# A spectral convolution and a cosine-like convolution on NHWC images: layer 1 with fixed homes for its blocks, an engine order tied to the step, and image statistics in thirds

## The chip, the cores and the metric

The kernel runs on one core of one Trainium2 chip. The metric is device time in microseconds (us), from one launch of the whole kernel. A core has five engines that run side by side, each through its own queue of instructions in a fixed order: TensorE (PE, with its weight loads shown apart as PEld), VectorE (DVE), ScalarE (ACT), GpSimd (POOL), and SyncE (SP), which here only issues DMAs. Engines wait for one another through semaphores. Data comes from DRAM into SBUF by DMA; PE writes its results to PSUM.

## The reference, cut to what matters

The input x has the shape (4, 512, 512, 16), float32. Two layers are added to it, each on a group-normalised input (8 groups of 2 channels, mean and variance over the whole image).

```python
# layer 0: a rational filter applied by a 1024 x 1024 FFT
x = x + _L0_conv_ref(_gn(x), L0_conv_h0, L0_conv_numerators, L0_conv_denumerator)
# layer 1: a 3 x 3 convolution, normalised like a cosine, through arccos
x = x + _L1_conv_ref(_gn(x), L1_conv_kernel, L1_conv_bias, L1_conv_radius)
...
    input_norm = sqrt(conv(x * x, ones) + EPS)        # 3 x 3 x C sum of squares
    kernel_norm = sqrt(sum(kernel * kernel) + EPS)
    y = conv(x, kernel / kernel_norm) / input_norm    # 'SAME'
    y = 1.0 - arccos(y) * (2.0 / pi)
    y = y * (tanh(kernel_norm / radius) * tanh(input_norm / radius))
    return y + bias
```

Only the end of layer 0 and layer 1 matter here.

## The kernel before, in words

The phases follow one another: filter, forward transform, the mixing of channels in the frequency domain, and `last_phase`, which holds the inverse transform along w, the statistics of layer 1, and layer 1 itself.

**The inverse transform.** 16 tiles of 16 rows each (256 row steps). A row step does eight matmuls into two PSUM tiles (lines 1163 and 1166), a copy on ACT (1169), two additions on POOL (1171 and 1172), three instructions on DVE (1173, 1176, 1177), and a DMA to DRAM. PSUM tiles have three buffers.

**The image statistics, `prepare`.** A generator that other loops advance by one stage at a time. It goes over the 64 places of 128 x 128 pixels (16 for each image), loads x (`p_x`, 1 MB) and layer 0's result (`p_y0` and `p_y1`, 0.5 MB each, eight channels in each) one place ahead, adds them on POOL (line 1098), takes one `bn_stats` for each channel on DVE (line 1094), and stores the sum (`t_d`). A place takes three calls: the add of channels 0 to 7; the add of channels 8 to 15 with the statistics of 0 to 7; the statistics of 8 to 15 with the store. After an image's 16 places come 16 aggregates and a chain of small operations through two matmuls, which leave the scale and shift `vec` of the image, in three more calls. The inverse transform calls it once every two row steps in its last seven tiles, so 56 times; 204 calls are needed in all.

**Layer 1.** An image is cut into groups of 32 columns (`xt`, 512 x 32 x 16), 16 for each image, 64 in all. A group has four blocks of 8 columns by 16 channels, with h in the free dimension (`block`: four transposes on PE, then Identity with scale and shift on ACT into `xn`, and Square into `x2`), and four units of 128 rows (`conv`: twelve matmuls over the group's four blocks and one for the columns of the neighbouring groups; each float32 matmul makes two records in the trace). There are 256 blocks and 256 units. A block has 512 elements and a zero on each side, which are the image's upper and lower border.

A step u of the loop works on many stages at once; what it issues, with line numbers, in the order of the code:

- `squares(u+13)`: four small matmuls of `x2` (1237) into one PSUM tile with a single buffer, and a copy to `sums` on DVE (1241), with copies on POOL of a group's outer column into its neighbour's (1243, 1246);
- every fourth step `norms`: three matmuls (1258 to 1260), the root and, every eighth step, tanh on ACT (1265, 1267; each change between tanh and the root loads a function table), a reciprocal on DVE (1269);
- `block(u+14)`: transposes (1211), the memset of the two border elements on POOL (1217), Identity (1219), Square (1221);
- every fourth step `border`: two copies on POOL (1287), four transposes (1290), two memsets on POOL, three instructions on DVE (1299);
- `conv(u+3)` (1307, 1315);
- `signed(u)` on POOL (1353) and `finish(u-1)`, the last addition on POOL (1367) with the output's DMA;
- `root(u+1)` (Abs, Relu, Sqrt; 1331 to 1333), `gate(u+1)` on POOL (1348), `factors(u+1)` (three squares and Sign; 1341 and 1343);
- `chain(u)`: five dependent instructions on DVE (1359 three times, 1360, 1362); the last one frees the unit's PSUM tile, of which there are four;
- `cosine(u+2)` on DVE (1325);
- every fourth step `over_w` on POOL (1250, 1251); then one call of `prepare`, if u is not negative.

The loop runs from u = -14 (`lead` is 14) to 256.

**What sets the order.** The framework records all instructions and then schedules them: each engine's queue is filled by a list scheduler that takes, among what it holds to be ready by its own estimate of time, what stands first in the program. So an instruction can be moved ahead of others that stand before it in the code. `InOrder` (line 213) is a helper that the kernel already uses in its filter phase: inside its `with` block, each instruction of the engines that it was given gets an edge from the one before it on the same engine, without a semaphore, so that the scheduler keeps the order of the code there. In layer 1 nothing is tied before the change. A tile from a pool is given to a buffer when one is free; the next tile in the same buffer waits for the last reader of the former.

```python
np_ = ctx.enter_context(tc.tile_pool(name="l_xn", bufs=16))
...
xn = np_.tile([P, N + 2], F32, name="xn")
nc.gpsimd.memset(xn[:, 0 : N + 2 : N + 1], 0.0)
vec = vecs[order[q // 64]]
nc.scalar.activation(xn[:, 1 : N + 1], pt, AF.Identity, scale=vec[:, 0:1], bias=vec[:, 1:2])
```

Of the kernel before, what the change touches and what calls it, by code (L numbers as in the profile page):

```python
# [40 lines left out]
F32 = mybir.dt.float32  # L41
# [5 lines left out]
P = 128  # L47
N = 512
# [160 lines left out]
def bc(ap, axis, shape):  # L209
    return ap.unsqueeze(axis).to_broadcast(shape)  # L210
# [758 lines left out]
def last_phase(tc, cst, x, y_d, yw_d, t_d, kern, bias, radius, out):  # L969
    nc = tc.nc  # L970
    with ExitStack() as ctx:
# [94 lines left out]
        def prepare():  # L1066


            places = [(b, w, h) for b in order for w in range(4) for h in range(4)]

            def load(b, w, h):
                t = pp.tile([P, P, C], F32, name="p_x")
                nc.sync.dma_start(out=t, in_=x[b, h * P : (h + 1) * P, w * P : (w + 1) * P, :])
                ys = []
                for jh in range(2):
                    y = pp.tile([P, C // 2, P], F32, name=f"p_y{jh}")
                    nc.sync.dma_start(
                        out=y, in_=yw_d[b][jh * C // 2 : (jh + 1) * C // 2, h * P : (h + 1) * P,
                                           w * P : (w + 1) * P].rearrange("j h w -> h j w"),
                    )  # L1080
                    ys.append(y)
                return t, ys

            ahead = load(*places[0])
            for at, (b, w, h) in enumerate(places):
                t, ys = ahead
                if w == 0 and h == 0:
                    stats = sm.tile([P, C, 16, 6], F32, name="l_stats")
                if at + 1 < len(places):
                    ahead = load(*places[at + 1])  # L1090

                def half(jh):
                    for j in range(8 * jh, 8 * jh + 8):
                        nc.vector.bn_stats(stats[:, j, 4 * w + h, :], t[:, :, j])

                def add(jh):
                    part = t[:, :, 8 * jh : 8 * jh + 8]
                    nc.gpsimd.tensor_add(part, part, ys[jh].rearrange("p j w -> p w j"))

                add(0)  # L1100
                yield
                add(1)
                half(0)
                yield
                half(1)
                nc.sync.dma_start(out=t_d[b][w][h * P : (h + 1) * P], in_=t)
                yield
                if w < 3 or h < 3:
                    continue

                mc = sm.tile([P, C, 2], F32, name="l_mc")
                for j in range(C):
                    nc.vector.bn_aggr(mc[:, j, :], stats[:, j].rearrange("p n s -> p (n s)"))
                nc.vector.tensor_sub(mc[:, :, 0], mc[:, :, 0], bias_b)
                pair = mc.rearrange("p (g k) s -> p g k s", k=2)
                mv = joined(nc, sm, pair[:, :, 0, :], pair[:, :, 1, :])
                mu = sm.tile([P, 8], F32, name="gn_mu")
                nc.vector.tensor_copy(mu, mv[:, :, 0])
                yield
                pm = ps_s.tile([P, 8], F32, name="gn_ps", tag="gn_ps")  # L1120
                nc.tensor.matmul(pm, mean_m, mu, start=True, stop=True)
                mean = sm.tile([P, 8], F32, name="gn_mean")
# [12 lines left out]
                nc.vector.scalar_tensor_tensor(both[:, 1], mean, -1.0, both[:, 0], ALU.mult, ALU.mult)  # L1135

                vec = sm.tile([P, 2], F32, name="l_vec", bufs=B)
                nc.vector.tensor_mul(both, both, bc(group, 1, [P, 2, 8]))
                nc.vector.reduce_sum(vec, both, axis=AX.X)
                nc.vector.scalar_tensor_tensor(vec[:, 1:2], vec[:, 0:1], bias_n, vec[:, 1:2],  # L1140
                                               ALU.mult, ALU.add)
                vecs[b] = vec
                yield
# [3 lines left out]
        with inner:  # L1147
            for n in range(16):
                b2, half, s8 = n // 8, n // 4 % 2, n % 4
# [33 lines left out]
                        next(beside, None)  # L1183

        xp = ctx.enter_context(tc.tile_pool(name="l_x", bufs=8))
        np_ = ctx.enter_context(tc.tile_pool(name="l_xn", bufs=16))
        ew = ctx.enter_context(tc.tile_pool(name="l_ew", bufs=2))
        ps_t = ctx.enter_context(tc.tile_pool(name="l_pst", bufs=2, space=PSUM))
        ps_c = ctx.enter_context(tc.tile_pool(name="l_psc", bufs=4, space=PSUM))
# [3 lines left out]

        n_groups = 16 * B
        n_units = 4 * n_groups
        borders, xt, xns, x2s, sums, pcs, rins, ths, st = ({} for _ in range(9))
        sh = [P, 32, C]

# [8 lines left out]
        def block(q):  # L1207

            pt = ps_t.tile([P, N], F32, name="pt")
            for h in range(4):  # L1210
                nc.tensor.transpose(
                    pt[:, h * P : (h + 1) * P],
                    xt[q // 4][:, h, q % 4 * 8 : q % 4 * 8 + 8, :].rearrange("p w c -> p (w c)"),
                    ident,
                )
            xn = np_.tile([P, N + 2], F32, name="xn")
            nc.gpsimd.memset(xn[:, 0 : N + 2 : N + 1], 0.0)
            vec = vecs[order[q // 64]]
            nc.scalar.activation(xn[:, 1 : N + 1], pt, AF.Identity, scale=vec[:, 0:1], bias=vec[:, 1:2])
            x2 = ew.tile([P, N], F32, name="x2")  # L1220
            nc.scalar.activation(x2, xn[:, 1 : N + 1], AF.Square)
            xns[q], x2s[q] = xn, x2
# [9 lines left out]
        def squares(q):  # L1232

            g, k = q // 4, q % 4
            p2 = ps_s.tile([P, 4, 8], F32, name="p2", tag="gn_ps")
            for h in range(4):
                nc.tensor.matmul(p2[:, h], x2s[q][:, h * P : (h + 1) * P], cols, start=True, stop=True)
            del x2s[q]
            if g not in sums:
                edges(g)  # L1240
            nc.vector.tensor_copy(sums[g][:, :, 1 + 8 * k : 9 + 8 * k], p2)
            if k == 0 and g % 16 > 0:
                nc.gpsimd.tensor_copy(sums[g - 1][:, :, 33:34], sums[g][:, :, 1:2])
            if k == 3 and g % 16 < 15:
                edges(g + 1)
                nc.gpsimd.tensor_copy(sums[g + 1][:, :, 0:1], sums[g][:, :, 32:33])
# [30 lines left out]
                    hi = 32 if ql == 0 and dh == 0 else min(8 * ql + 9, 32)  # L1277
                    yield 4 * g + ql, dh, lo, hi, lo - (8 * ql - 1)

        def border(g):  # L1280

            t = ew.tile([P, 4, 3, 2, C], F32, name="e_bx")
            for side in range(2):
                at, w = (g + 2 * side - 1, 31 - 31 * side)
                if at // 16 != g // 16 or at < 0:
                    at, w = g, 0
                nc.gpsimd.tensor_copy(t[:, :, :, side], bc(xt[at][:, :, w, :], 2, [P, 4, 3, C]))
            pt = ps_t.tile([P, N], F32, name="pt")
            for h in range(4):
                nc.tensor.transpose(pt[:96, h * P : (h + 1) * P],  # L1290
                                    t[:, h].rearrange("p d s c -> p (d s c)"), ident)
            bx = ew.tile([96, N], F32, name="e_bn")
            nc.gpsimd.memset(bx[0:32, 0:1], 0.0)
            nc.gpsimd.memset(bx[64:96, N - 1 : N], 0.0)
# [28 lines left out]
        def cosine(u):  # L1323
            y = ew.tile(sh, F32, name="e_y", bufs=4)
            nc.vector.tensor_mul(y, pcs[u], bc(rins[u // 4][:, u % 4, :], 2, sh))  # L1325
            st["y", u] = y
# [44 lines left out]
        lead = 14  # L1371

        def step(u):
# [7 lines left out]
                norms(g)  # L1381
            if u + lead < n_units:
                block(u + lead)
            if u % 4 == 2 and 0 <= u + 6 < n_units:
                border((u + 6) // 4)
            if 0 <= u + 3 < n_units:
# [8 lines left out]
                factors(u + 1)  # L1395
            if 0 <= u < n_units:
                chain(u)
            if 0 <= u + 2 < n_units:
                cosine(u + 2)
            g, k = divmod(u + lead - 2 - 4, 4)  # L1400
            if k == 0 and 0 <= g < n_groups:
                over_w(g)
# [6 lines left out]
            next(beside)  # L1409
        for g in range(3):  # L1410
            load(g)
        for u in range(-lead, n_units + 1):
            step(u)


def body(tc, ins, cst, out):
# [47 lines left out]
```

## Time and profile before

| | us |
|---|---|
| median of three runs | 16199.08 (16192.73 to 16224.64) |
| the profiled execution, its own time | 16219.56 |
| its span, first to last instruction | 16217.8 |
| inverse transform without statistics, 13600 to 13800 | 73 row steps |
| inverse transform with statistics, 13800 to 14300 | 148 row steps |
| first block of layer 1 (line 1211) | 14387.8 |
| first instruction of chain(0) (line 1359) | 14436.6 |
| last statistics load issued (line 1073) | 15467.5 |
| end of the span | 16217.8 |

Over the whole span PE is busy 91%, DVE 66%, ACT 55%, POOL 65%, at a mean granted clock of 0.969. Layer 1 is only its last ninth: of 40 slices of 405 us it fills the last four and a half. Times inside the trace are counted from the start of the span. A line of the trace gives its start, its length, the engine, the source line, the operation, the tiles (what is written, an arrow, what is read), the shape and the number of instructions merged into the line. Lengths of neighbouring records overlap by up to 0.1 us, since an engine starts the next instruction before the last one's end is recorded; so the distance between starts tells what an instruction costs. In a list of waits, a line names the engine and line that waited, the one that it waited for, the sum in us, how often, and the longest.

### The profile page before, as it was taken

The page shows a single profiled execution, that of the slowest core. Times are in us where ns is not written, and L with a number is a line of the kernel's source. Part 1 is how long each engine was busy: PE and PEld are TensorE (multiplying, and loading weights), DVE is VectorE, ACT ScalarE, POOL GpSimd, SP SyncE. Part 2 cuts the span into 40 slices and gives each one's busy share as a digit, 9 for nine tenths or more (in the row PEclk, how much of TensorE's full clock was granted, in tenths as well). Part 3 has the DMA queues.
Part 4 walks back from the last instruction along what each step waited for, and adds up shares of the span by engine and source line. Part 5 has one row for each costly group of instructions (what it writes and reads, how often), then busy time and mean ns, then how long its engine had stood idle before and what let it go on. Part 6 is the DMA issues. An engine that isn't in the chain of part 4 may idle for free. (4 is left out here: it accounts for less than half of the span.)

```text
span 16217.8 us, 539020 instructions
## 1 busy us (share of the span) xinstructions
PE 14720.9 (91%) x232588; PEld 10874.5 (67%) x232588; DVE 10679.6 (66%) x21019; ACT 8839.0 (55%) x17007; POOL 10556.5 (65%) x10157
## 2 busy tenths in 40 slices
PE   7999999999988888888888888888888889888898
PEld 5555555554557666667676676677676767777787
DVE  8999999993545555555555555555555555778877
ACT  4666666663345555555555555555555553147788
POOL 7777777772356666666666666666666665667766
PEclk8999999999999999999999999999999999989899
DMA  4888888888878888888888888888888888975521
GB/s 138 239 244 246 244 245 239 244 242 259 251 271 329 326 330 329 330 329 326 329 327 328 330 327 329 326 324 330 329 329 330 328 330 305 326 253 196 197 103 66
DMA packets 2917339, 4542.72 MB, mean 280 GB/s; under 512 B 125730, under 2 KB 2094076, under 8 KB 2805262
## 3 DMA queue, kind: packets, MB, share of 16 engines
q1 hardware_dynamic: 2705758, 3836.11, 68.6%
q0 software_dynamic: 172336, 605.00, 9.4%
q10 hardware_dynamic: 36864, 67.13, 1.2%
q8 instruction: 1830, 29.98, 0.7%
q14 instruction: 551, 4.51, 0.1%
HBM read 3030.45 MB, written 1477.31 MB: 278 GB/s over the span
## 5 line engine op out<-in xcount | busy, mean ns | idle before, releaser
L848 PEld LDWEIGHTS pm<-xe,gh 128*32 128x32 f32 x131328 | 1996.9, 111 | 1437.8 <-issue 1141.2
L848 PE MATMUL pm<-xe,gh 128*32 128x64 f32 x131328 | 2366.9, 222 | 649.6 <-issue 320.2
L832 PE MATMUL pg<-c_dg,g 64*128 64x128 f32 x32832 | 2607.1, 290 | 311.9 <-ACT gh L732 195.8
L877 DVE TENSOR_TENSOR z<-zq,pz 128x256 f32<-128x256 f32 x2052 | 860.0, 419 | 2956.7 <-ACT zq L876 2952.5
L832 PEld LDWEIGHTS pg<-c_dg,g 64*128 64x128 f32 x32832 | 2143.6, 191 | 575.4 <-ACT gh L732 245.2
L732 ACT COPY gh<-pg 128x512 f32<-128x512 f32 x2567 | 1447.8, 585 | 1302.8 <-PE pg L832 1299.9
L462 PE MATMUL pt<-ev_in,c_todd 128*128 128x512 f32 x4096 | 1924.9, 609 | 9.1 <-DMA ev_in<-g_d 9.0
L392 DVE RECIPROCAL dn<-dn 128x256 f32<-128x256 f32 x1024 | 1722.9, 1724 | 17.6
L393 POOL TENSOR_TENSOR sp<-m,dn 128x512 f32<-128x512 f32 x1024 | 1301.4, 1271 | 592.0 <-DVE dn L392 555.2
L812 ACT COPY xe<-xl 64x1024 f32<-64x1024 f32 x513 | 539.0, 1051 | 1868.9 <-POOL xl L803 1868.9
L730 DVE COPY gh<-pg 128x512 f32<-128x512 f32 x1537 | 1055.4, 687 | 661.0 <-PE pg L832 658.4
L869 PE MATMUL pz<-c_ident,yf 128*128 128x128 f32 x8208 | 1378.5, 291 | 18.5 <-issue 11.6
L801 POOL TENSOR_TENSOR xu<-xe,c_late 128x256 f32<-128x256 f32 x2052 | 1374.5, 694 | 21.7 <-DVE xe L730 6.9
L462 PEld LDWEIGHTS pt<-ev_in,c_todd 128*128 128x128 f32 x4096 | 729.1, 190 | 909.9 <-issue 772.9
L421 ACT COPY st<-pg 128x256 f32<-128x256 f32 x2048 | 617.0, 390 | 1300.9 <-PE pg L410 1300.9
L410 PEld LDWEIGHTS pg<-c_dinv,sp 64*128 64x128 f32 x16384 | 1005.5, 196 | 442.1 <-ACT sp L398 232.6
L803 POOL TENSOR_TENSOR xl<-xl,xu 128x1024 f32<-128x1024 f32 x513 | 1209.2, 2357 | 40.2
L1307 PE MATMUL pc<-l_band,xn 128*128 128x160 f32 (+2 forms) x6144 | 1112.8, 341 | 70.7 <-DVE e_o L1362 70.1
L410 PE MATMUL pg<-c_dinv,sp 64*128 64x128 f32 x16384 | 1108.1, 287 | 60.3 <-ACT sp L398 44.6
L885 POOL TENSOR_TENSOR zd<-z 128x512 f32<-128x512 f32 x513 | 654.5, 1276 | 778.8 <-DVE z L877 778.8
L917 POOL DMA_DIRECT2D y_d<-yo x511 | 296.5, 580 | 1275.9 <-ACT yo L732 1250.3
L906 PE MATMUL py<-z,c_ig 128*64 128x256 f32 x6156 | 1120.5, 396 | 6.5 <-issue 2.7
(216 smaller groups left out, 30900.2 us busy)
## 6 DMA issues: line engine op xcount, KB each, us to landing
xe<-xf_d SPq DMA_DIRECT2D x1026, 1536.0 KB
g<-g_d SPq DMA_DIRECT2D x511, 1024.0 KB
g_d<-st SPq DMA_DIRECT2D x256, 1024.0 KB
ev_in<-g_d SPq DMA_DIRECT2D x1024, 256.0 KB
g_d<-ot SPq DMA_DIRECT2D x1024, 256.0 KB
xf_d<-xe POOLq DMA_DIRECT2D x513, 448.0 KB, 8.2
xf_d<-xl POOLq DMA_DIRECT2D x513, 448.0 KB, 6.3
x_d<-xo SPq DMA_DIRECT2D x128, 1024.0 KB
```

The costliest lines, as they stand in the source:

```text
L392: nc.vector.reciprocal(dn, dn)
L393: nc.gpsimd.tensor_mul(w["sp"][:, v], w["m"][:, v], bc(dn, 2, [P, 2, 2, P]))
L410: nc.tensor.matmul(pg[u][:, n, k].rearrange("p a x -> p (a x)"), w["sp"][q, n, k, c, :], dinv[q, 2 * kp + k, c, :], start=(c == 0), stop=( ...
L462: nc.tensor.matmul(pt, todd[:, c, kc, hh * P : hh * P + P], ev[:, kc, c], start=(kc == 0), stop=(kc == 1),)
L732: nc.scalar.copy(dst, src)
L801: nc.gpsimd.tensor_mul(u[:, :, h, c], xe[:, :, h, 1 - c], bc(late[:, 1 + c], 2, [P, F, 2]))
L803: nc.gpsimd.tensor_add(xl.rearrange("p f h c k -> p (f h c k)"), xl.rearrange("p f h c k -> p (f h c k)"), u.rearrange("p f h c k -> p (f ...
L832: nc.tensor.matmul(pg[c][:, j % 4], g[half, j], dg[half], start=True, stop=True)
L848: nc.tensor.matmul(pm[32 * q : 32 * q + 32, g % 8], gh[:, f].rearrange("p c j -> p (c j)"), xe[:, :, f].rearrange("p t h c k -> p t (h c k ...
L869: nc.tensor.transpose(pz[:, t % 4].rearrange("p v q x -> p (v q x)"), y[:, at].rearrange("p g x -> p (g x)"), ident)
L906: nc.tensor.matmul(py[64 * half : 64 * half + 64, odd], ig[:, s0, c2], zs.rearrange("p (t h) j -> p h t j", h=2), start=(c2 == 0), stop=(c ...
L1307: nc.tensor.matmul(pc[:, lo:hi, :].rearrange("p w j -> p (w j)"), xns[q][:, h * P + dh : h * P + dh + P], bands[dh][:, o : o + hi - lo, :] ...
```

## The change

- The 16 homes of normalised blocks become 16 tiles of their own, made once, and their border elements are set to zero once. `block(q)` writes into home q modulo 16. The 256 memsets become 16.
- Every step of layer 1's loop is put into an `InOrder` block for PE, DVE, ACT and POOL. SP is left to the scheduler.
- Three helpers are cut in two, so that a part can stand elsewhere in the step: the POOL copies of `border` become `ends`, one step earlier; the memsets and DVE rows of `border` become `borders_in`, after `chain`; the neighbour copies of `squares` become `across`, after `cosine`.
- A place of the statistics is cut into 6, 5 and 5 channels in place of 8 and 8. The adds of a place are 0 to 5; 6 to 7 and 8 to 10; 11 to 15. The statistics are 0 to 5, 6 to 10 and 11 to 15, each one call after its add; the last third falls into the first call of the next place. The store stays in the third call.

```diff
-                add(0)
+                add(0, 6)
                 yield
-                add(1)
-                half(0)
+                add(6, 8)
+                add(8, 11)
+                sums(0, 6)
                 yield
-                half(1)
+                add(11, 16)
+                sums(6, 11)
                 nc.sync.dma_start(out=t_d[b][w][h * P : (h + 1) * P], in_=t)
                 yield
+                sums(11, 16)
...
-        np_ = ctx.enter_context(tc.tile_pool(name="l_xn", bufs=16))
+        np_ = ctx.enter_context(tc.tile_pool(name="l_xn", bufs=1))
...
+        ring = [np_.tile([P, N + 2], F32, name=f"xn{n}") for n in range(16)]
+        for t in ring:
+            nc.gpsimd.memset(t[:, 0 : N + 2 : N + 1], 0.0)
...
-            xn = np_.tile([P, N + 2], F32, name="xn")
-            nc.gpsimd.memset(xn[:, 0 : N + 2 : N + 1], 0.0)
+            xn = ring[q % 16]
...
+
+        def across(q):
+            g, k = q // 4, q % 4
             if k == 0 and g % 16 > 0:
                 nc.gpsimd.tensor_copy(sums[g - 1][:, :, 33:34], sums[g][:, :, 1:2])
...
+            if u % 4 == 1 and 0 <= u + 7 < n_units:
+                ends((u + 7) // 4)
             if u % 4 == 2 and 0 <= u + 6 < n_units:
                 border((u + 6) // 4)
...
             if 0 <= u < n_units:
                 chain(u)
+            if u % 4 == 2 and 0 <= u + 6 < n_units:
+                borders_in((u + 6) // 4)
             if 0 <= u + 2 < n_units:
                 cosine(u + 2)
+            if 0 <= u + lead - 1 < n_units:
+                across(u + lead - 1)
...
+        tied = InOrder(tc, nc.tensor, nc.vector, nc.scalar, nc.gpsimd)
         for u in range(-lead, n_units + 1):
-            step(u)
+            with tied:
+                step(u)
```

More of the change, by code (lines that the diff above doesn't have):

```diff
@@ L1090, in prepare, with sums, add @@
                     ahead = load(*places[at + 1])
-                def half(jh):
-                    for j in range(8 * jh, 8 * jh + 8):
+                def sums(lo, hi):
+                    for j in range(lo, hi):
                         nc.vector.bn_stats(stats[:, j, 4 * w + h, :], t[:, :, j])
-                def add(jh):
-                    part = t[:, :, 8 * jh : 8 * jh + 8]
-                    nc.gpsimd.tensor_add(part, part, ys[jh].rearrange("p j w -> p w j"))
-                add(0)
+                def add(lo, hi):
+                    jh = lo // 8
+                    part = t[:, :, lo:hi]
+                    nc.gpsimd.tensor_add(part, part, ys[jh][:, lo - 8 * jh : hi - 8 * jh].rearrange("p j w -> p w j"))
+                add(0, 6)
                 yield
-                add(1)
-                half(0)
+                add(6, 8)
+                add(8, 11)
+                sums(0, 6)
                 yield
-                half(1)
+                add(11, 16)
+                sums(6, 11)
                 nc.sync.dma_start(out=t_d[b][w][h * P : (h + 1) * P], in_=t)
                 yield
+                sums(11, 16)
                 if w < 3 or h < 3:
@@ L1278, in terms, with ends @@
                     yield 4 * g + ql, dh, lo, hi, lo - (8 * ql - 1)
-        def border(g):
+        def ends(g):
             t = ew.tile([P, 4, 3, 2, C], F32, name="e_bx")
@@ L1287, in border @@
                 nc.gpsimd.tensor_copy(t[:, :, :, side], bc(xt[at][:, :, w, :], 2, [P, 4, 3, C]))
+            st["bx", g] = t
+        def border(g):
+            t = st.pop(("bx", g))
             pt = ps_t.tile([P, N], F32, name="pt")
@@ L1291, in border, with borders_in @@
                                     t[:, h].rearrange("p d s c -> p (d s c)"), ident)
+            st["pb", g] = pt
+        def borders_in(g):
+            pt = st.pop(("pb", g))
             bx = ew.tile([96, N], F32, name="e_bn")
```

## The prediction

> **What bounds the kernel now.** First the table by stage. The stretches are the 148 units of layer 1 that run beside the image statistics (chain(0) starts at 14436.6, chain(147) ends at 15534), the next 95, and the last 13. The statistics calls are counted in the code: 51 for image 0, 56 spent in the inverse transform, 204 in all, so 148 are left, one a step.
>
> ```profile
> core 0: us, PE busy (x) PEld busy (x) DVE busy (x) ACT busy (x) POOL busy (x), PEclk, DMA share, GB/s
> 14436.00:15533.00 1097.00, 931.10 (x6000) 816.30 (x6000) 902.89 (x1947) 844.05 (x1434) 833.36 (x972) 0.90 0.57 190
> 15533.00:16156.00 623.00, 572.50 (x3842) 508.54 (x3842) 464.88 (x767) 530.60 (x910) 387.82 (x565) 0.93 0.22 75
> 16156.00:16218.00 62.00, 43.92 (x280) 38.31 (x278) 50.59 (x82) 51.83 (x88) 45.72 (x41) 0.89 0.16 60
> ```
>
> A unit takes 1098/148 = 7.42 us beside the statistics and 623/95 = 6.56 after them. No engine is full: the first stage has DVE at 82%, PE at 85%, ACT at 77%, POOL at 76%. So order is the bound. The waits between 14500 and 16000 say which:
>
> ```profile
> DVE e_sum L1241 <- PE p L1237: 199.0, 114, 9.5
> ACT xn L1219 <- POOL xn L1217: 118.0, 23, 10.2
> ACT xn L1219 <- PE pt L1211: 104.1, 45, 6.3
> PEld pc L1307 <- DVE e_o L1362: 69.9, 64, 4.0
> POOL e_bx L1287 <- PE pt L1290: 69.2, 29, 5.2
> ```
>
> DVE stands at the 0.19 us copy of the squares; ACT stands behind the two-column memset, which itself waits for a convolution to give up its block; PE stands until the chain of an earlier unit frees an accumulator. Each is an instruction placed too early in a queue.
>
> Third, what a unit costs when an engine never waits. Start-to-start distances matter, since records overlap. PE at full clock:
>
> ```profile
> 15779.11 1.04 PE L1237 MATMUL p<-c_cols,x 128*128 128x8 f32 x8
> ...
> 15780.36 3.88 PE L1307 MATMUL pc<-l_band,xn 128*128 128x512 f32 x24
> 15784.08 0.29 PE L1315 MATMUL pc<-l_eband,e_bn 96*128 96x16 f32 x2
> 15784.22 1.04 PE L1237 MATMUL p<-c_cols,x 128*128 128x8 f32 x8
> ```
>
> 5.11 us, plus a quarter of the border transposes (0.6) and of the six norm records (about 1.2): **PE 5.56**.
>
> **DVE in the tied order.** The new order lets the chain run as five instructions that each need the one before. Their distance, against that of instructions with something independent between:
>
> ```profile
> 15723.99 1.49 DVE L1359 SCALAR_TENSOR_TENSOR pc<-e_q,pc 128x512 f32<-128x512 f32 x2
> 15725.51 0.69 DVE L1360 SCALAR_TENSOR_TENSOR pc<-e_v,pc 128x512 f32<-128x512 f32 x1
> 15726.29 0.69 DVE L1362 SCALAR_TENSOR_TENSOR e_o<-pc,e_gate 128x512 f32<-128x512 f32 x1
> ...
> 14728.50 0.38 DVE L1094 BATCH_NORM_STATS2 l_stats<-p_x 128x6 f32<-128x128 f32 x1
> 14728.79 0.68 DVE L1362 SCALAR_TENSOR_TENSOR e_o<-pc,e_gate 128x512 f32<-128x512 f32 x1
> 14729.38 1.49 DVE L1094 BATCH_NORM_STATS2 l_stats<-p_x 128x6 f32<-128x128 f32 x5
> 14730.80 0.17 DVE L1241 COPY e_sum<-p 128x32 f32<-128x32 f32 x1
> ```
>
> Dependent: 0.76 (the last 0.78). Independent: 0.60. A statistics instruction: 1.42/5 = 0.284. So a step is copy 0.11 + 3 x 0.76 + 0.78 + e_o 0.60 + cosine 0.60 = 4.37; border 2.37/4 = 0.59; reciprocal 0.86/4 = 0.22: 5.18 us. The old order hides 4 x 0.16 of it behind statistics. Statistics left at chain(0): 768 less 22 = 746 x 0.284 = 212. An image's end: 16 aggregates 7.3 plus some 5 of small operations, three times: 37. Sum: 148 x 5.18 + 212 + 37 = **1016 us against 1098: -82**. Does anything stop DVE? Counted from the start of DVE's step u: convolution u+2, which cosine needs, ended about 5 before it; squares u+13, which the copy needs, about 4 before; Sign u, which signed needs, about 4 before, and signed is done 1.3 later, e_o only at 3.2. POOL needs signed 1.28 + finish 1.27 + gate 1.10 + adds (two 2.87 and two extra starts: 5.9 a place, 1.97 a step) + small copies about 0.6 = 6.2, under DVE's 6.86. So DVE sets the step.
>
> **The stage after.** DVE 5.18, POOL 4.2. ACT in its new order: Identity to Square 0.79 and Abs to Relu to Sqrt 0.65 each, because each needs the one before (0.52 where it doesn't), three arcs 1.84, the others 0.52: 5.49. The two table loads per eight units:
>
> ```profile
> 16156.43 0.62 ACT L1331 ACTIVATE e_v<-e_y 128x512 f32<-128x512 f32 x1
> 16157.06 1.28 ACT L1267 ACT_TABLE_LOAD   x1
> 16158.36 0.51 ACT L1267 ACTIVATE l_th<-l_inn,l_rrad 128x256 f32<-128x256 f32 x1
> ...
> 16159.93 1.28 ACT L1333 ACT_TABLE_LOAD   x1
> ```
>
> with tanh 3.0/8 and the root of the norms 0.07: **ACT 5.95**. PE: the row grants 0.93 in this stage and PE was busy 572.5/95 = 6.03 a unit. The Trainium skill, "TensorE: Matmul & The Clock Gate", Part 1, says the clock halves after an idle window of about 3.4 us and returns after as busy a one; a tied order has no wait of that length, so by the rule the clock goes to 1.0, PE to 5.56, and ACT bounds: 95 x 5.95 = 565, -58. By the row PE bounds: 95 x 6.03, -50. I take 6.1, nearer the row: 580, **-43**.
>
> **Start and end.** Squares of a block are tied ahead of the next block's transposes, so before the convolutions begin one block is in flight: transposes 0.6, Identity 0.77, Square 0.62, squares 1.04, gaps: 3.3 warm; the eight squares took 1.85 on the cold clock at 14395.75, so 4.7 cold. The old order started convolution pieces at 14397 and ran blocks ahead. I take 4.0 x 10 steps, then three steps with convolutions at 6.2: chain(0) near 14458, **+22** (10 to 35). End: 13 x 4.45 for 56 us between 16156 and 16212: **+2**.
>
> **Adds in thirds, in the inverse transform.** 73 units of it took 200 us before the statistics join, 148 took 500 after: 2.74 and 3.38. Beside an add of 2.98 us at 14340.24 the DVE instruction of line 1177 took 3.01, its median neighbour 0.47. The Trainium skill, "GPSIMD Engine Reference", section 1, names the cause: the SBUF interface is shared, and a DVE instruction with two SBUF inputs contends. By the rule the blocked time is the adds' total, unchanged: 0. By the row the longest block falls from 2.9 to about 2.1, and three PSUM buffers cover more of it; PE waited 91 us for DVE here, a fifth of which would be 18. I take **-5** (-18 to +10).
>
> **Edits at nothing.** 240 of 256 memsets go (25 us of POOL, not the bound); their home is free two steps early, since the last reader of block u-2 is convolution u+1, tied into step u-2. Ends (two copies, 0.35 us each) moves a step earlier, ahead of signed on POOL: e_o has 1.9 us to spare there. The three border rows move behind the chain on DVE: their PSUM bank is held some 4 us longer, and its next user comes two steps on; the convolution reads them three steps on. The neighbour copies (0.19) move behind gate on POOL and wait for DVE's squares copy of their own step, with the adds queued behind them and statistics one step later waiting for those; the sum over w has the copy right before it, and PE's norms want that sum two steps on. The squares' bank is single, as before: PE waits for the last step's copy, 5 us old by then. If these covers go, POOL's 0.6 a step is what is left. SP isn't tied: a place's p_x waits for the statistics one step later than before, but has two to three steps (13 to 20 us) to land.
>
> **Sum**: -82 - 43 + 22 + 2 - 5 = -106. The steps aren't equal: each eighth has 3 us more of ACT and 2 of PE. I estimate 1 us lost in each of 30: +30. Forecast **-76** on this execution's 16219.6. The runs' median is 20 lower, 16199; their spread is 32. The forecast is against the median: **16124 us**.
>
> **Rivals.**
> - *Better than that*: no loss in uneven steps, start at +10, inverse transform at -18: -82 - 58 + 10 + 2 - 18 = -146, 16053. For it: every cross-engine need is a step old. Against: 0.09 us of slack between PE and ACT in the last stage. Chance 0.14.
> - *No change*: the queue of DVE waits for what it now meets in a fixed order. For it: the same page's Part 1 calls ACT and DVE strict first-in, first-out, so a waiting head stops all behind it, which speaks against tying; the old order had the same queues and chose its places. With 0.35 us a step of such waits over 243 steps, +85 in place of +30: -21, 16178. Chance 0.15.
> - *Slower: POOL's add meets its load.* SP sends p_y1 only after the previous place's store, which waits for that place's last add; the new add(8,11) comes about two steps (11 to 13 us) later. If it has not landed, POOL stops, with signed, e_o, and PE's accumulator behind it. POOL has 0.6 a step, 1.9 a place; 46 places. A wait of 4.5 us a place costs 46 x 2.6 = 120: +44, 16243. It turns the sign from (76/46) + 1.9 = 3.6 us a place. For it: POOL waited 41 us for p_x in 18 places of this stage, at most 3.8. Against: DMA is 57% busy. Chance 0.16.
> - *The order doesn't bind the engines*: not counted, since the block encloses every instruction of a step.
>
> The forecast's own case has 0.55; its range is 16085 to 16165. The bounds of the unknown costs and the rivals widen it to 16045 to 16225. A measurement of this kernel tells 0.2% (32 us) from no change: faster than 16167: 0.68; between 16167 and 16231: 0.16; slower: 0.16.
>
> **What would show it.** Right: no L1217 line under ACT's waits; chain(0) later by 10 to 35; in the first stage DVE over 92% busy at 6.9 us a unit with its wait for the squares nearly gone; after it 6.1 a unit, ACT or PE over 93%, the clock above 0.95. Wrong: POOL waiting for p_x or p_y more than 80 us; DVE below 88%; PE waiting for x (Square) every step; a start over 50 us late.

## The result, and the profile after

The changed kernel takes 16113.7 us (median of 4 runs, 16106.75 to 16131.15) against 16206.72 for the kernel before (16192.73 to 16224.64): a ratio of 0.9944, with a 95% interval from 0.993 to 0.9957. The profiled execution took 16131.15 us, 88.4 less than that of before (16219.56).

The table by stage of the changed kernel, in the columns that the prediction showed: the inverse transform, the stretch from its last row to chain(0), the 148 units beside the statistics, the next 95, and the end.

```profile
core 0: us, PE busy (x) PEld busy (x) DVE busy (x) ACT busy (x) POOL busy (x), PEclk, DMA share, GB/s
13542.00:14371.00 829.00, 724.28 (x4113) 653.39 (x4109) 594.00 (x1091) 153.22 (x261) 500.22 (x605) 0.94 0.87 312
14371.00:14446.50 75.50, 52.36 (x271) 45.96 (x272) 11.33 (x26) 25.62 (x37) 5.37 (x20) 0.62 0.36 132
14446.50:15475.00 1028.50, 905.83 (x5968) 805.44 (x5967) 967.50 (x2015) 877.47 (x1420) 882.13 (x924) 0.91 0.66 214
15475.00:16063.00 588.00, 552.39 (x3878) 493.89 (x3877) 476.57 (x770) 565.42 (x923) 379.15 (x477) 0.98 0.22 79
16063.00:16129.00 66.00, 43.70 (x269) 38.11 (x267) 55.89 (x83) 54.31 (x88) 46.26 (x45) 0.84 0.15 56
```

Each stretch has one engine that is near to full now: DVE 967.5 of 1028.5 us in the third line (94%, before 82%), and ACT 565.4 of 588 in the fourth (96%, before 85%). The work is nearly the same as before, but DVE has 2015 instructions in the third line where it had 1947. For differences the two traces have to be cut at the same instructions: at the first of chain(0) and at the line that writes e_o in units 147 and 242. Cut like this the first stage took 1097.2 us before and takes 1030.9 now, the stage after it 623.9 and 583.7. Two stretches became longer: the start from 48.5 to 75.4 us, at a clock of 0.62, and the end from 60.1 to 68.1.

The waits of the two stages (the engine and line that waited, the one it waited for, the sum, how often, the longest), first of the stage beside the statistics, then of the one after it:

```profile
POOL e_gate L1369 <- ACT e_y L1359: 112.5, 52, 7.2
ACT xn L1225 <- PE pt L1218: 92.3, 31, 13.0
PE pc L1323 <- DVE e_o L1378: 73.9, 50, 2.1
```

```profile
POOL e_gate L1369 <- ACT e_y L1359: 204.4, 96, 6.3
DVE l_rin L1278 <- ACT l_inn L1274: 49.9, 24, 3.0
DVE e_sum L1247 <- PE p L1243: 13.5, 16, 1.6
```

Of the three waits that the prediction pointed at, two are gone. DVE's for the squares' copy was 176.3 us between 14500 and 15900 and is 11.2 there. ACT's for the memset has no line. The third grew: PE's wait for an accumulator from DVE was 36.5 us in the first stage and is 73.9. Most of what is left stands at engines that are not full in that stage: POOL waits for Sign, ACT for transposes, PE for DVE.

One step on DVE beside the statistics, by start, length, line and tiles:

```profile
15003.12 0.19 DVE L1247 COPY e_sum<-p 128x32 f32<-128x32 f32 x1
15003.23 2.29 DVE L1375 SCALAR_TENSOR_TENSOR pc<-e_q,pc 128x512 f32<-128x512 f32 x3
15005.55 0.69 DVE L1376 SCALAR_TENSOR_TENSOR pc<-e_v,pc 128x512 f32<-128x512 f32 x1
15006.33 0.69 DVE L1378 SCALAR_TENSOR_TENSOR e_o<-pc,e_gate 128x512 f32<-128x512 f32 x1
15006.94 0.68 DVE L1341 TENSOR_TENSOR e_y<-pc,l_rin 128x512 f32<-128x512 f32 x1
15007.54 1.52 DVE L1094 BATCH_NORM_STATS2 l_stats<-p_x 128x6 f32<-128x128 f32 x5
15008.98 0.17 DVE L1247 COPY e_sum<-p 128x32 f32<-128x32 f32 x1
```

This is the predicted order, with no wait in it, and the predicted distances: 2.32 for three dependent instructions, 0.78 to e_o, 0.61 from e_o to the cosine. The step lasts 5.86 us from copy to copy.

The start is the predicted loop as well. DVE's copies of the squares, one for each block, each with its wait in brackets:

```profile
14386.47 0.19 DVE L1247 COPY e_sum<-p 128x32 f32<-128x32 f32 x1 [4.17 <-PE p L1243]
14390.89 0.19 DVE L1247 COPY e_sum<-p 128x32 f32<-128x32 f32 x1 [4.22 <-PE p L1243]
14395.30 0.19 DVE L1247 COPY e_sum<-p 128x32 f32<-128x32 f32 x1 [4.22 <-PE p L1243]
```

4.41 us a block: transposes, Identity, Square and the squares' matmuls one after another.

What the prediction did not see is where the statistics went. The `bn_stats` of line 1094 alone, first of the kernel before, then of the changed one, each over the inverse transform, the start up to the first e_o, and the next 147 units:

```profile
13542.00:14388.30 846.30, 102.67 (x334) 0.92 0.89 317
14388.30:14442.80 54.50, 5.15 (x18) 0.78 0.58 208
14442.80:15534.00 1091.20, 217.47 (x672) 0.90 0.58 191
```

```profile
13548.00:14371.50 823.50, 85.98 (x278) 0.94 0.87 313
14371.50:14449.90 78.40, 0.00 (x0) 0.63 0.34 126
14449.90:15478.00 1028.10, 222.04 (x746) 0.91 0.66 215
```

Of the 1024, 256 belong to image 0. The kernel before did 352 ahead of the first e_o and the changed one 278, so the old order had pulled 74 of them forward (56 into the inverse transform), and the tie put them back into layer 1. In the inverse transform the two kernels agree up to row 240 (769.5 and 766.3 us, with 262 and 263 statistics). The last 16 rows took 64 us before, with 72 statistics among them, and take 45 with 15. DVE's time for the 56 is 16.7 of the 22.8 us by which the rows are shorter. The first stage carries these statistics now.

### The profile page after: what moved, and what is told of

It reads as the page before. It is cut to its first block, busy times and chain, and to the rows that moved or that the text cites. A ratio compares the mean times of both kernels' runs of the same rounds, so it can differ in the third digit from the quotient of the medians.

```text
span 16129.4 us, 538678 instructions
## 1 busy us (share of the span) xinstructions
PE 14669.9 (91%) x232588; PEld 10842.1 (67%) x232588; DVE 10725.4 (66%) x21019; ACT 8903.5 (55%) x17007; POOL 10592.6 (66%) x10045
## 5 line engine op out<-in xcount | busy, mean ns | idle before, releaser
L869 PE MATMUL pz<-c_ident,yf 128*128 128x128 f32 x8208 | 1375.7, 291 | 15.8 <-issue 10.1
L410 PE MATMUL pg<-c_dinv,sp 64*128 64x128 f32 x16384 | 1107.9, 287 | 59.4 <-ACT sp L398 44.6
```

Source lines behind the costliest of these rows:

```text
L410: nc.tensor.matmul(pg[u][:, n, k].rearrange("p a x -> p (a x)"), w["sp"][q, n, k, c, :], dinv[q, 2 * kp + k, c, :], start=(c == 0), stop=( ...
L869: nc.tensor.transpose(pz[:, t % 4].rearrange("p v q x -> p (v q x)"), y[:, at].rearrange("p g x -> p (g x)"), ident)
```

## The experiments

Twelve kernels ran. Stages are from each run's profile, in us: "rows" from the first to the last of the inverse transform's 256 rows, "start" from there to the first e_o, "units" from the first e_o to the last (255 units). The time at which the inverse transform starts isn't shown: it moved between 13516.7 and 13566.9 though no run changed what lies ahead of it, so the stages tell small effects better than the medians do. But they come from one execution each: up to row 240 of the inverse transform, where no edit but the thirds matters, eight kernels took from 758 to 771 us.

| run | rows | start | units | median | ratio to before, 95% |
|---|---|---|---|---|---|
| before | 834.7 | 54.7 | 1768.6 | 16206.7 | 1 |
| changed | 811.9 | 78.6 | 1673.1 | 16113.7 | 0.9944 (0.993 to 0.9957) |
| e1 thirds only | 832.7 | 59.4 | 1775.4 | 16216.6 | 1.0004 (0.9995 to 1.0013) |
| e2 homes only | 823.2 | 58.1 | 1755.6 | 16203.6 | 0.9993 (0.9984 to 1.0002) |
| e3 all but the tie | 831.5 | 49.5 | 1770.4 | 16216.7 | 1.0001 (0.9992 to 1.001) |
| e4 all but thirds | 813.4 | 77.5 | 1676.2 | 16128.6 | 0.9947 (0.993 to 0.9963) |
| e5 tie only | 808.3 | 78.8 | 1772.8 | 16231.2 | 1.0016 (1.0006 to 1.0025) |
| e6 statistics in the chain | 808.1 | 79.0 | 1647.1 | 16088.1 | 0.9924 (0.9909 to 0.9939) |
| e7 ACT's order | 808.8 | 79.0 | 1655.7 | 16107.7 | 0.9936 (0.9921 to 0.9951) |
| e8 start untied | 809.1 | 61.2 | 1672.7 | 16123.8 | 0.9944 (0.9929 to 0.9958) |
| e9 all but homes | 814.9 | 78.7 | 1680.7 | 16110.8 | 0.9942 (0.9927 to 0.9957) |
| e10 tie and homes | 815.2 | 78.7 | 1736.5 | 16181.0 | 0.9977 (0.9967 to 0.9986) |
| e11 e6, image ends late | 812.0 | 78.6 | 1626.3 | 16065.1 | 0.9912 (0.9897 to 0.9927) |
| e12 e11, e7 and e8 together | 808.8 | 62.0 | 1582.1 | 16000.2 | 0.9867 (0.9853 to 0.9882) |

The medians were taken against three sets of runs of the kernel before (medians 16214.4, 16210.15 and 16213.16, beside the 16206.72 of the result).

### One part alone: thirds, homes, and all but the tie

e1 is the kernel before with the statistics in thirds; e2 the kernel before with the homes:

```diff
-        np_ = ctx.enter_context(tc.tile_pool(name="l_xn", bufs=16))
+        np_ = ctx.enter_context(tc.tile_pool(name="l_xn", bufs=1))
...
-            xn = np_.tile([P, N + 2], F32, name="xn")
-            nc.gpsimd.memset(xn[:, 0 : N + 2 : N + 1], 0.0)
+            xn = ring[q % 16]
```

> Before, with the statistics in 6, 5 and 5 channels and nothing else. Theory A (the adds' length is what holds DVE up in the inverse transform; layer 1's gain is from the tie): the inverse transform falls from 853 us to about 829, as in the changed kernel, layer 1 stays within 10 us of before (48 us to its first chain, 1098, 622, 62): 16180, -24. Rival B (POOL's total is the same, so the shorter inverse transform came from elsewhere): the inverse transform stays at 850, no change, 16205. Rival C (thirds are what evens out layer 1): layer 1's first stage falls by 40 or more: 16130.

> Before, with the sixteen homes made once and their borders zeroed once, and nothing else: 240 memsets less, no tie. Theory A: the 118 us that ACT stood behind the memset were the scheduler's placing; with the memset gone ACT's Identity waits for the last convolution of its home itself or for the transposes, and layer 1 keeps its order's losses: between -25 and +10, 16180 to 16215. Rival D (the memset's wait was the loss, since each wait stood in ACT's queue): layer 1 loses 60 to 118 us of waits, 16090 to 16150.

e3 is the changed kernel, its steps no longer tied:

```diff
-            with tied:
-                step(u)
+            step(u)
```

> The changed kernel without the tie: homes, thirds, moved helpers, but the scheduler places the instructions. Theory A: the start of layer 1 comes back to 50 us (-25), the inverse transform stays at 829, both long stages go back to 7.2 to 7.4 and 6.4 to 6.6 us a unit (+70 and +35): 16190, near before. Rival D (homes and moved helpers do it): at or under the changed kernel, 16085 to 16115.

None of the three medians can be told from the kernel before (in its one trace e2 is shorter by 13 us of units and 11 of rows). In e3 homes, thirds and moved helpers are all there, the memset is gone, and still DVE waits 100.6 us for the squares in the first stage (before 127.7 in the same stretch). So none of the gain comes without the tie. Taking away the memset, the second largest wait of the old profile, mostly let other waits take its place: in e2 ACT waits 127.7 us for its transposes in the first stage, before 64.9.

### The tie without thirds

e4 is the changed kernel with the places cut into 8 and 8 channels again.

> The changed kernel with the statistics in 8 and 8 channels again, tied. Theory A: DVE and POOL have the same totals in layer 1, so its first stage is 0 to 15 us longer (steps of 0, 8, 8 statistics, 2.3 us apart from the mean, partly taken up by the 4 us of lead that the other engines have); the inverse transform is 24 longer: 16137 to 16155. Rival C (under a tie uneven statistics stall the step): the first stage is 40 to 80 us longer: 16180 to 16220.

Rows, start and units agree with the changed kernel within 3.1 us; the 24 us that theory A took off the rows for the thirds are not there. No effect of thirds shows in either order: the rows are 834.7 against 832.7 untied, and 813.4 against 811.9 tied. So the shorter inverse transform (-23 us) comes from the tie; e5, the tie alone, has it as well. The count of statistics in the last 16 rows shows most of the way that it takes.

### The tie alone, and what it needs

e5 is the kernel before and nothing but the tie:

```diff
+        tied = InOrder(tc, nc.tensor, nc.vector, nc.scalar, nc.gpsimd)
         for u in range(-lead, n_units + 1):
-            step(u)
+            with tied:
+                step(u)
```

> Before, with the tie around each step and nothing else: a memset for each block, border and neighbour copies where they were, 8 and 8 channels. Theory A (what counts is that each engine keeps the step's order; the other edits only keep the leads): POOL's copies of the border now stand in the same step as their transposes, so PE loses some 5 us of lead every fourth step, and Identity waits for a memset that stands behind the last step's adds; DVE keeps most of its full queue: within 40 us of the changed kernel, 16115 to 16155. Rival F (the moved helpers and the homes are what makes a tie bearable): one wait of 2 us or more in each step, 243 steps less what lead covers: 16250 to 16500, slower than before.

It brings no gain: the median is 0.16% above before, which lies between the two theories. The traced execution, the fastest of its ten, has rows, start and units that together are 2 us longer than before. Its stage after the statistics is 14 us shorter than before (609.8), but its first stage, counted over 147 units, takes 1103 us, 12 longer, with these waits. The second view has one of them in POOL's timeline:

```profile
ACT xn L1219 <- POOL xn L1217: 190.5, 87, 8.0
POOL e_sum L1243 <- DVE e_sum L1241: 143.8, 35, 12.8
PE pt L1290 <- POOL e_bn L1293: 98.8, 36, 10.4
```

```profile
14818.21 1.06 POOL L1348 TENSOR_TENSOR e_gate<-l_th,l_ktn 128x512 f32<-128x512 f32 x1
14825.32 0.19 POOL L1243 COPY e_sum<-e_sum 128x4 f32<-128x4 f32 x1 [6.05 <-DVE e_sum L1241]
14825.44 0.11 POOL L1217 MEMSET xn<- 128x2 f32 x1
14825.50 1.28 POOL L1353 TENSOR_TENSOR e_gate<-e_gate,e_y 128x512 f32<-128x512 f32 x1
```

A 0.19 us copy stands at the head of POOL's step and waits for DVE's copy of the same step; the memset is behind it, ACT's Identity behind the memset, and PE's border transposes wait for POOL in the same way. Of the twelve steps that make a pattern one takes 12.4 us and another 11.1.

Two more kernels tell apart which cure counts. e9 is the changed kernel with pooled blocks and their memsets, the helpers staying where they were moved to; e10 is e5 with the homes, the helpers uncut.

> The changed kernel, tied and with the helpers where it moved them, but the normalised blocks come from a pool again and each has its two-column memset on POOL ahead of the step's signed. It tells which of the two, homes or moved helpers, the tie needs. Theory H (the moved helpers are what it needs; the memset waits only for POOL's adds of the step before, and the loop memset, Identity to Sign 5.5 us, signed, finish, gate and add 6.0 us, spread over two steps, gives 5.8 us a step, under the step's 6.9): 16110 to 16150, ACT waits under 60 us for the memset. Theory F (the homes are what it needs: ACT stands behind a memset that stands behind POOL's queue in every step): 16180 to 16240, ACT waits over 150 us for the memset.

> The kernel before with the homes and the tie, but border and squares uncut and where they stood. Theory H (the moved helpers are what the tie needs: POOL's neighbour copies wait at the head of the step for DVE's squares copy, and PE's border transposes wait for POOL in the same step): 16170 to 16230, POOL waits over 120 us for the copy of the squares, and every fourth step takes over 10 us. Theory F (homes are what it needs): 16110 to 16150.

The first stage's waits of e9 and of e10:

```profile
ACT xn L1223 <- POOL xn L1221: 25.7, 54, 1.1
```

```profile
POOL e_sum L1245 <- DVE e_sum L1243: 135.4, 33, 12.8
...
PE pt L1292 <- POOL e_bn L1295: 104.4, 36, 10.5
```

With the helpers moved, the memset waits are at most 1.1 us, and e9 is as fast as the changed kernel. With the homes but without the moves POOL still stops for DVE, and 63 us of the units' 96 are missing. The homes do save 36 there (1772.8 to 1736.5). ACT no longer stands behind the memset, but waits 160.0 us for its transposes instead (18.6 in e5), so the path of these 36 us is not shown. So the gain needs two parts, the tie and the helpers put behind their waits; given these, homes or thirds can go, each alone. A kernel without both of them was not run, and which of the three moved helpers counts was not tested: the waits name the neighbour copies and the border.

### What is left in the tied order

e6 puts the statistics between the dependent instructions of the chain, where DVE would otherwise stand for 0.16 us; the call of the statistics moves ahead of the chain, and the next load's issue to the end of the step:

```diff
                 nc.vector.scalar_tensor_tensor(r, q, rest, r, ALU.add, ALU.mult)
+                if pend:
+                    pend.pop(0)()
```

> The changed kernel with one statistics instruction between every two of the chain, in the same tied step (the call of the statistics stands before the chain; what is left follows cosine). Theory A (DVE sets the first stage's step, and a dependent instruction costs 0.16 us more than an independent one): 4 x 0.16 = 0.64 us less in each of about 139 steps, down to POOL's 6.2: first stage 1029 to between 940 and 960, the rest as it was: 16025 to 16050. Rival G (POOL's adds, the loads or PE at a clock of 0.91 set the step as well): at most 20 us less: 16095 or more.

A step of e6 on DVE:

```profile
14608.25 0.17 DVE L1266 COPY e_sum<-p 128x32 f32<-128x32 f32 x1
14608.34 0.68 DVE L1394 SCALAR_TENSOR_TENSOR pc<-e_q,pc 128x512 f32<-128x512 f32 x1
14608.93 0.38 DVE L1396 BATCH_NORM_STATS2 l_stats<-p_x 128x6 f32<-128x128 f32 x1
14609.23 0.67 DVE L1394 SCALAR_TENSOR_TENSOR pc<-e_q,pc 128x512 f32<-128x512 f32 x1
14609.82 0.37 DVE L1396 BATCH_NORM_STATS2 l_stats<-p_x 128x6 f32<-128x128 f32 x1
```

The pair takes 0.89 us where dependent chain and statistics took 0.76 + 0.28 = 1.04; the step from copy to copy is 5.08 us in place of 5.86. Yet the units gain only 26 us, and the median, 16088, lies between the ranges of the two theories. Twelve steps take 76.9 us against 80.3, so something else sets some of them: DVE waits for ACT's root of the norms and for the squares again (27.0 and 16.2 us in the stage). The three steps around an image's end take 38 to 41 us against 32 to 34: the chain stands behind the 16 aggregates there. e11 puts the image ends back behind the chain:

```diff
+                later.append(lambda: res.append(end1()))
                 yield
```

> e6 (statistics put between the chain's instructions), but the three calls at the end of an image (16 aggregates and the small operations, three times in this stage) stand at the end of their step, behind chain and cosine, as in the changed kernel. In e6 a block of 12 steps took 76.9 us against the changed kernel's 80.3, which is 6.41 against 6.69 us a unit and would give 41 us over 148 units, but the three steps at an image's end took 39 us there against 32 before. Theory A (the chain stood behind the aggregates, so e_o and PE's accumulators came late): 16055 to 16075, the three steps back to about 32 us. Theory B (the aggregates cost the same wherever they stand, now that DVE has no slack): 16080 to 16095, the three steps stay at 39.

It gains 21 us of units more, inside theory A's range. At one image end the three steps took 33, at the two others 32 (15.6 + 6.6 + 10.0) and 33.

e7 is the changed kernel with ACT's instructions in another order, so that few need the one just before them. `root` keeps Abs, `square` is the Square taken out of `block`, and `root2` does Relu, Sign and Sqrt:

```diff
                 root(u + 1)
+            if u + lead < n_units:
+                square(u + lead)
+            if 0 <= u + 1 < n_units:
+                root2(u + 1)
                 gate(u + 1)
```

> The changed kernel with ACT's step in the order Identity, Abs, Square, Relu, Sign, Sqrt, three arcs, so that no instruction stands right behind the one that it needs. Theory A (ACT sets the stage after the statistics, 565 of 588 us busy): 0.39 us less of ACT a unit; PE's 5.8 a unit (552/95) bounds next: second stage 588 to between 550 and 570; first stage the same, since DVE sets it: 16085 to 16105. Rival H (PE sets that stage): second stage 580 to 590, and 0.5 us later squares cost PE something: 16110 to 16135.

ACT's step, in the changed kernel and in e12, which has this order:

```profile
15703.65 0.76 ACT L1225 ACTIVATE xn<-pt,l_vec 128x512 f32<-128x512 f32 x1
15704.45 0.63 ACT L1227 ACTIVATE x<-xn 128x512 f32<-128x512 f32 x1
...
15709.18 0.76 ACT L1225 ACTIVATE xn<-pt,l_vec 128x512 f32<-128x512 f32 x1
```

```profile
15701.10 0.76 ACT L1253 ACTIVATE xn<-pt,l_vec 128x512 f32<-128x512 f32 x1
15701.76 0.62 ACT L1378 ACTIVATE e_v<-e_y 128x512 f32<-128x512 f32 x1
15702.28 0.62 ACT L1258 ACTIVATE x<-xn 128x512 f32<-128x512 f32 x1
15702.80 0.62 ACT L1383 ACTIVATE e_v<-e_v 128x512 f32<-128x512 f32 x1
...
15706.20 0.77 ACT L1253 ACTIVATE xn<-pt,l_vec 128x512 f32<-128x512 f32 x1
```

From Identity to Identity 5.10 us in place of 5.53. Over 95 units that would be 41 us, but the stage gained only 14 (583.7 to 570.1): PE is busy 549 us of it, 96%, which makes it the likely next bound. The median, 16107.7, is just above theory A's range.

e8 leaves the steps below u = -3 untied:

```diff
+            if u < -3:
+                step(u)
+                continue
             with tied:
                 step(u)
```

> The changed kernel with the steps before the first convolution (u under -3) not tied. Theory A (the start's 75 us is the loop transposes, Identity, Square, squares, 4.4 us a step with one block in flight, which the tie alone makes): blocks and squares overlap again, start 50 to 60 us: 16090 to 16100. Rival I (the start waits for its loads and for the cold clock): 70 to 75 us as before: 16110 to 16120.

The start falls from 78.6 to 61.2 us (to the first of chain(0): 75.4 to 58.1, inside theory A's range), but the median doesn't show it and misses both ranges. In the profiled execution the inverse transform began 18 us later than in the changed kernel; whether it did so in the others is not known.

e12 has e11, e7 and e8 together.

> All that gained so far together: statistics between the chain's instructions with the image ends at the end of the step, ACT's instructions in another order (Identity, Abs, Square, Relu, Sign, Sqrt, three arcs), and the first steps (u below -3) left untied. Theory A (the three work in different stages, so they add: about -50, -14 and -17): 16015 to 16050. Theory B (in the first stage DVE, POOL and PE all come near to full, so the parts hide one another, and the start is lost again in filling the pipeline): 16050 to 16080.

It beats both kernels: its median is 113 us below that of the changed one, and its ratio to before is 0.9867 (0.9853 to 0.9882). It lies below the range that theory A gave. The table of its two stages:

```profile
14412.00:15362.00 950.00, 854.55 (x5950) 766.83 (x5949) 915.44 (x2012) 831.81 (x1418) 876.45 (x917) 0.96 0.70 232
15362.00:15930.00 568.00, 547.40 (x3866) 490.03 (x3865) 470.20 (x762) 533.05 (x917) 379.56 (x477) 0.98 0.23 82
```

The first stage fell by 78 us against the changed kernel, where statistics in the chain (e11) took 47 off it and ACT's order alone 4. So the parts helped one another. The likely reason, not tested apart, is that in e11 ACT (busy 872 us of 980) and PE set some of the steps once DVE was shorter. The waits agree: DVE's for ACT's root of the norms fell from 25.0 us in e11 to 13.0, its wait for the squares from 16.8 to 10.2. PE's clock rose as well, from 0.93 in e11 to 0.96, which may be cause or effect. Now DVE is at 96% and POOL at 92%.

## Why the prediction was right, step by step

The direction, the main mechanism and the size came out: 16124 was forecast and 16113.7 measured, inside the likeliest case's own range. The fall itself is larger than forecast, 93 us between the medians where 75 were forecast. Against the profiled execution's own time -76 was summed, and it is -88.4, with both traces cut at the same instructions:

| term | predicted | measured |
|---|---|---|
| first stage, 148 units | -82 | -66 |
| stage after, 95 units | -43 | -40 |
| uneven steps | +30 | in the two above |
| start | +22 | +27 |
| end | +2 | +8 |
| inverse transform | -5 | -23 |
| all phases ahead of it, unchanged | 0 | +6 |

- **DVE bounds the first stage: right.** 1016 was the sum of its instructions; the stage took 1030.9, which leaves 15 for uneven steps. The count of 746 statistics is exactly what the trace of the changed kernel has.
- **The stage after: right in kind.** ACT's sum of 565 stands against 562.8 us busy of 583.7, and the clock rose from 0.93 to 0.98. The prediction took this from the rule on the clock ("TensorE: Matmul & The Clock Gate", Part 1: the clock halves after an idle window of about 3.4 us). The outcome agrees with it, the reason doesn't: in this stage no stretch without a matmul was longer than 1.85 us in the kernel before, and the clock fell to half for 3.4 us at a time all the same; the longest now is 1.38. That the clock came out as the rule had it is in part luck. Both stages together came to -106, against -95 with the allowance of 30, which was some 12 too large.
- **Start: right in kind, its sum not.** 4.41 us a block against 4.0 assumed, and e8 takes most of the loop's cost away. But the terms that the prediction gives, 10 steps at 4.0 and three at 6.2 from the first block at 14387.8, end at 14446, which is +10, not +22. Measured are 71.6 us from the first block to chain(0): 7.0 for the first block, which the terms leave out, 45.4 for ten more and 18.7 for three.
- **End: too small.** The steps of the end were given +2; in the tied order they cost +8. Why was not looked into.
- **Inverse transform: the term that failed.** "Adds in thirds" was given -5, between 0 by the rule and -18 by the row. e1 and e4 show no effect of thirds in either order (2.0 and 1.5 us of rows). This fits 0; that the blocked time is the adds' total was the prediction's own reading of "GPSIMD Engine Reference", section 1, which names only the shared interface. The -23 come from the tie. The prediction had counted that 746 statistics were left for the first stage, and took it for no change; it had not asked how many were left before. In the kernel before, 672 lay there. The tie moved 74, at 0.284 us some 21 us, into the first stage: 56 from the inverse transform and 18 from the start. Only the price was in the sum.
- **"Edits at nothing": right as a sum, wrong as a judgement.** The moved helpers add little wait, as predicted (POOL waits 14.8 us for the squares' copy in the first stage, in two lines of 10.1 and 4.7). But the text said that without this cover POOL's 0.6 us a step would be what is left. e10 shows 63 us of units lost where the helpers stay put, and e5 all of the gain. The places of the helpers are as needed as the tie, and the homes, which removed ACT's most visible wait, are dispensable once the helpers are moved: e9.
- **The rivals.** POOL's add meeting its load: POOL waited 9.3 us for p_x and 9.5 for p_y over the whole trace, which is 0.4 us for each of 46 places, against the 3.6 that would have turned the sign. Queues waiting in a fixed order (the page behind that rival's first-in, first-out queues is "TensorE: Matmul & The Clock Gate", Part 1): little of it in this kernel, but it is what e5 and e10 have, so its mechanism was real, on POOL's queue more than on DVE's, and the moved helpers are what kept it away.

## What to carry to other kernels

When no engine is full and the waits point at tiny instructions, as here, suspect the order. Here pinning it helped only where, in the pinned order, each instruction that needed another engine's work of the same step stood behind what didn't; test the pin without the moves, and the moves without the pin, before crediting either. When an order is pinned, count also what the free scheduler had pulled ahead into an earlier stage, in both stages. After it, look at the new full engine for instructions that each need the one before, and put independent work between them; do this for two engines that are near to full together, since one alone mostly uncovers the other: here the two alone took 47 and 4 us off the first stage, and together 78.

## What the runs showed of the hardware

- An engine that is never out of work still loses time to dependence. On DVE a 128x512 instruction that needs the one before it starts 0.76 us after it, and with independent work behind it 0.60; on ACT 0.65 to 0.80 against 0.52 to 0.66. The Trainium skill ("VectorE: DVE Perf Modes", "The DRAIN you can't avoid") says that the next operation doesn't start until the pipe is empty, that eight copies took the same time with a semaphore after each as with one after the last, and that an operation which isn't held starts earlier. Here the distance does depend on whether the next one needs the last; in this kernel such an instruction also waits for the semaphore of the one before it, and the two can't be told apart. Putting statistics into the gaps took 47 us off a stage of 1028 (e11).
- PE's clock can stay down without a long pause. In the changed start it stood at half from 14373.1 to 14431.2, where PE was busy about 36 of 58 us in a loop of 4.41 us a block. PE stood idle for 5.8 and 4.0 us up to 14380.2; from there on no stretch without a matmul was longer than 1.6 us, and the clock stayed at half for 51 us more.
- The time at which the inverse transform starts moved over 50 us between profiled executions of kernels whose program is the same up to there, 0.3% of the whole. What causes it stays open.
